# A graph layer on one core: the head's order on three engines, later node loads behind the edge list, paired stores, and GNN weights loaded in the adjacency

## The chip, the cores and the metric

The kernel runs on one core of one Trainium2 chip. The metric is device time in microseconds (us). The kernel before took 1140.14 us, the median of three runs (1139.82 to 1141.01). The engines are named as the profile names them: PE is TensorE (PEld its weight loads), DVE is VectorE, ACT is ScalarE, POOL is GpSimd, SP is SyncE, which here only issues transfers. ACTq and SPq are the transfer-issuing sides of ACT and SP.

## The reference, cut to what matters

One layer of a graph network for N = 3125 nodes of C = 256 numbers and E = 103,125 directed edges, sorted by destination. `xn` is the layer norm of `x`. The GNN part, the part that the change touches:

```
agg  = segment_sum(xn[src], dst, N)
h    = relu(agg @ W_rel + b_rel + xn @ W_root)
g    = h @ W_ih.T + b_ih + b_hh;  i, f, g, o = split(g, 4)
gnn  = (sigmoid(o) * tanh(sigmoid(i) * tanh(g))) @ W_fc + b_fc
x    = x + gnn + mix(xn)           # mix: per-head k'v attention, heads of 32
x    = x + ffn(layernorm(x))       # top 2 of 8 experts, 256 -> 1024 -> 256
```

## The kernel before, in words

Nodes lie in 25 tiles of P = 126 rows, five tiles to a batch (five batches, b = 0 to 4) and four to a root group (seven groups, r = 0 to 6, the last of one tile). The program has four stages: the head, the adjacency, the GNN, and the experts.

**The head** does two things at once.

*The edge list.* `dst` and `src` lie on the chip as 128 x 808 integers (`raw`). `find()` (L237) casts them on ACT (L248), transposes them on PE (L254), copies them out on ACT (L258, L261) and stores them to DRAM as `ends_dram` with two transfers issued by ACT (L263, 768 KB; L265, 42 KB). Meanwhile DVE counts for each of 525 groups of six destinations how many first entries of `firsts` lie below its limit (L275, five passes), which gives `at_i`. POOL gathers five blocks `near` with it (L283), DVE refines the position to `begin_i` (L289, L292), POOL gathers five blocks `both` of 256 edges per group (L297), DVE turns them into a key and a source row (L307 to L316), and checks the order of the list (L321, L322, L324). PE sums the check (L326), transposes the keys (L336), ACT writes `rowT` (L338) and DVE `keyT` (L340).

*The nodes.* `norm(b)` (L345) takes the moments of five tiles on DVE (L194, L195), a square root on ACT (L197, `rs`), a reciprocal and five scalings on DVE (L198, L349), and stores `xn_dram`. `rounded(b)` (L354) makes `hi`, the rounded copy, on ACT (L356); DVE makes `lo`, the rest (L436). `root(t0)` (L358) transposes four tiles on PE (L366, 8 transposes), copies them to `xt` on ACT (L368, two copies), multiplies by W_root on PE (L373: 8 matmuls of 504 columns, which the trace shows as 16), evacuates each of four results on ACT with the bias (L376, `hr`), and stores `xT_dram` (504 KB) and `root_dram` (four stores of 252 KB).

**The adjacency.** `build()` (L379) makes 18 columns of a 126 x 25 x 252 block A of the adjacency matrix: two comparisons on DVE (L384, `hr` and `hk`), six small matmuls on PE (L390), a cast on ACT (L392). A chunk needs 14 such banks. The comparisons have two buffers, so DVE is at most two banks ahead of PE. The first block, A0, is built in the head; PE begins chunk 0 of the aggregation (L631) when all 14 banks of A0 are there, and during chunk c builds the block for c + 1. There are 13 chunks. `fetch`, `means` and so on (L509 to L563) put the mix part between the banks.

**What sets the order.** Each engine runs its instructions in the order in which the compiled program has them. That order is chosen by the scheduler of the Tile framework, from the order in the source and from `tc.issue_after(ins)`, which puts what is written inside it behind `ins`. Every transfer issued by SP or ACT signals its end on one of eight semaphores, taken in turn by both queues together; before a transfer is issued, its queue waits until the transfer that had this semaphore before, the eighth before it in that turn, has landed. In the kernel before, the second list store (L265) has the semaphore of the first node batch, `xn` b = 0. Behind it on ACT stand the table load and the `rs` of that batch.

SP's order in the head before: `raw` (two loads), `xn` b = 0, `wroot`, `firsts`, `brel`, `xn` b = 1 to 4, `behind`, then twelve small loads (`wcol` to `of`), then the stores of the head with the loads of the GNN weights (L445 `wrel`, L450 `wih`, L452 `wfc`, 4 MB in all) among the last of them.

Of the kernel before, what the change touches and what calls it, by code (L numbers as in the profile page):

```python
# [9 lines left out]
F32 = mybir.dt.float32  # L10
# [3 lines left out]
AF = mybir.ActivationFunctionType  # L14
OP = mybir.AluOpType
# [3 lines left out]
C = 256  # L19
P = 126  # L20
# [43 lines left out]
def gps_layer(  # L64
# [35 lines left out]
    xT_dram = dram.tile([128, KC, NP], F32, name="xT_dram")  # L100
    root_dram = dram.tile([128, KH, NP], F32, name="root_dram")
# [13 lines left out]
    def load_nodes(to, t0, t1):  # L115

        if t1 == T:
            nc.vector.memset(to[:, T - 1 - t0, :], 0.0)
            nc.sync.dma_start(to[:LAST, T - 1 - t0, :], x[(T - 1) * P:N, :])
            t1 = T - 1  # L120
        if t1 > t0:
            nc.sync.dma_start(to[:, :t1 - t0, :], tiles_of(x, t0, t1))
# [32 lines left out]

    nc.sync.dma_start(raw[:, 0, :], dst)
    nc.sync.dma_start(raw[:, 1, :], src)
    for b in range(T // TB):
        load_nodes(xn[:, b * TB:(b + 1) * TB, :], b * TB, (b + 1) * TB)
        if b == 0:  # L160
            nc.sync.dma_start(wroot, W_root.rearrange("(k p) m -> p k m", p=128))
            nc.sync.dma_start(firsts, dst[0:1, :].to_broadcast([GP, NCP]))
            brel = columns_of(b_rel, KH, "brel")

    nc.sync.dma_start(behind[:112, :], dst[1:113, :])
    nc.sync.dma_start(behind[111:127, :], dst[112:, :])
    nc.sync.dma_start(behind[127:, :NCP - 1], dst[0:1, 1:])
# [48 lines left out]

    wcol = gw.tile([128, 2, KC], F32, name="wcol")
    for i, ap in enumerate((kln_w, kln_b)):
        nc.sync.dma_start(wcol[:, i, :], ap.rearrange("(k p) -> p k", p=128))
    wrow = gw.tile([128, 2, KC, 128], F32, name="wrow")  # L220
    for i, ap in enumerate((vln_w, vln_b)):
        nc.sync.dma_start(wrow[:, i].rearrange("p k c -> p (k c)"), rows_of(ap, C, 128))
    bfc = gw.tile([P, 1, C], F32, name="bfc")
    nc.sync.dma_start(bfc[:, 0, :], rows_of(b_fc, C, P))
    bg = columns_of(b_ih, 4 * KH, "bg").rearrange("p (g k) -> p g k", g=4)
    bg2 = columns_of(b_hh, 4 * KH, "bg2").rearrange("p (g k) -> p g k", g=4)
    wr = gw.tile([128, KC, NE], F32, name="wr")
    nc.sync.dma_start(wr, Wr.rearrange("(k p) e -> p k e", p=128))
    brb = gw.tile([P, 1, NE], F32, name="brb")
    nc.sync.dma_start(brb[:, 0, :], rows_of(br, NE, P))  # L230
    small = gw.tile([128, KS, NE], F32, name="small")
    ofs = [columns_of(ap, NE * k, f"of{k}{i}")
           for i, (ap, k) in enumerate(((ln_g, KC), (ln_b, KC), (b1, KF)))]

    total_i = const.tile([128, 1], I32, name="total_i")

    def find():  # L237
# [8 lines left out]
        for i in range(2):  # L246
            ends = sp.tile([128, NCP], F32, name="ends", tag="ends", bufs=2)
            nc.scalar.copy(ends, raw[:, i, :])  # L248
            for r in range(0, nr, 4):
                pt = ps_tr()  # L250
                m = min(4, nr - r)
                for j in range(m):
                    w = min(128, NCP - 128 * (r + j))
                    nc.tensor.transpose(pt[:w, 128 * j:128 * j + 128],  # L254
                                        ends[:, 128 * (r + j):128 * (r + j) + w], ident)
                whole_ = m if NCP >= 128 * (r + m) else m - 1
                if whole_:
                    nc.scalar.copy(rows[:, r:r + whole_, :, i],  # L258
                                   pt[:, :whole_ * 128].rearrange("p (r e) -> p r e", e=128))
                if whole_ < m:  # L260
                    nc.scalar.copy(rows[:left, r + whole_, :, i],  # L261
                                   pt[:left, whole_ * 128:m * 128])
# [10 lines left out]
        scr = sp.tile([GP, NCP], F32, name="scr", tag="ends", bufs=2)  # L273
# [18 lines left out]
        nc.vector.scalar_tensor_tensor(begin_i, at, 128.0, below, op0=OP.mult, op1=OP.add)  # L292
# [27 lines left out]
        order = sp.tile([128, NCP], F32, name="order", tag="ends", bufs=2)  # L320
# [3 lines left out]
        nc.vector.tensor_reduce(wrong[:, 1:2], full, AX.X, OP.add)  # L324
# [7 lines left out]
        for q in range(GQ):  # L332
            pt = ps_tr()
            for o, of in enumerate((g_src, key)):
                for h in range(GH):
# [4 lines left out]
            nc.vector.tensor_scalar(keyT[:, q * GP:(q + 1) * GP, :],  # L340
                                    pt[:, GH * GP:2 * GH * GP].rearrange("p (h g) -> p g h", h=GH),
                                    off, None, op0=OP.add)
# [15 lines left out]
    def root(t0):  # L358
# [10 lines left out]
        nc.sync.dma_start(xT_dram[:, :, t0 * P:t0 * P + n], xt[:, :, :n])  # L369
        for m in range(KH):  # L370
            pm = ps_mm()
            for k in range(KC):
                nc.tensor.matmul(pm[:, :n], wroot[:, k, 128 * m:128 * m + 128], xt[:, k, :n],  # L373
                                 start=(k == 0), stop=(k == KC - 1))
            hr = np_.tile([128, TQ * P], F32, name="hr", bufs=6)
            nc.scalar.activation(hr[:, :n], pm[:, :n], AF.Identity, bias=brel[:, m:m + 1])  # L376
            nc.sync.dma_start(root_dram[:, m, t0 * P:t0 * P + n], hr[:, :n])
# [25 lines left out]

    pins = []
    steps = find()
    next(steps)
    with tc.issue_after(pins.pop().ins):
        normed = norm(0)
    with tc.issue_after(normed.ins):
        next(steps)  # L410
    root(0)
    rounded(0)
    with tc.issue_after(pins.pop().ins):
        norm(1)
    next(steps)
    nc.vector.tensor_copy(two[:, 0], two_f[:, :, None].to_broadcast([128, DT, GH]))
    root(TQ)
    rounded(1)
    norm(2)
    root(2 * TQ)  # L420
    rounded(2)
    for _ in steps:
        pass
    norm(3)
    rounded(3)
    norm(4)
    rounded(4)
# [3 lines left out]
    root(3 * TQ)  # L431
    for _ in range(2):
        next(parts)
    for b in range(T // TB):
        u = slice(b * TB, b * TB + TB)
        nc.vector.tensor_tensor(lo[:, u, :], xn[:, u, :], hi[:, u, :], OP.subtract)  # L436
    for t0 in range(4 * TQ, T, TQ):
        root(t0)
        for _ in range(5):
            next(parts, None)  # L440
    nodes.close()
# [3 lines left out]
    nc.sync.dma_start(wrel, W_rel.rearrange("(k p) m -> p k m", p=128))  # L445
    wih = gl.tile([128, KH, 3, DH], F32, name="wih")

    wv = W_ihT.rearrange("(k p) m -> p k m", p=128)
    for i, gate in enumerate((0, 2, 3)):
        nc.sync.dma_start(wih[:, :, i, :], wv[:, :, gate * DH:(gate + 1) * DH])  # L450
    wfc = gl.tile([128, KH, C], F32, name="wfc")
    nc.sync.dma_start(wfc, W_fc.rearrange("(k p) m -> p k m", p=128))  # L452

# [6 lines left out]
    nc.sync.dma_start(wr_dram, wrT)  # L460

# [127 lines left out]
    def inputs(t0):  # L589
# [3 lines left out]
        nc.sync.dma_start(xT[:, :, :n], xT_dram[:, :, t0 * P:t0 * P + n])  # L593
        root = inp.tile([128, KH, TQ * P], F32, name="root", bufs=1)
        nc.sync.dma_start(root[:, :, :n], root_dram[:, :, t0 * P:t0 * P + n])
# [13 lines left out]
    with tc.tile_pool(name="odd", bufs=1) as op_:  # L609
        As = [A0, op_.tile([P, T, AC], F32R, name="A1")]  # L610
        for c, (d0, d1) in enumerate(chunks):
# [26 lines left out]
            for k in range(KC):  # L638
                nc.scalar.copy(aggT[:, k, d0:d1], pg[k][:, :n])  # L639
            if c == 2 * nb_ + 1:  # L640
# [542 lines left out]
```

## Time and profile before

| stretch of the profiled execution, us from the span's start | PE busy | DVE busy | ACT busy |
|---|---|---|---|
| 0 to 17.17, up to the first root matmul | 5.50 of 17.17 | 7.14 | 8.68 |
| 17.17 to 50.30, up to the check of the list (L326) | 27.63 of 33.13 | 25.82 | 12.91 |
| 50.30 to 59.04, up to the end of the last keyT | 5.11 of 8.74 | 8.38 | 3.60 |
| 59.04 to 97.03, up to the first matmul of chunk 0 | 35.06 of 37.99 | 19.46 | 21.17 |
| 97.03 to 116.00, chunk 0 | 18.38 of 18.97 | 16.73 | 7.58 |
| 116.00 to 324.80, chunks 1 to 10 | 198.20 of 208.80 | 169.08 | 128.13 |
| 324.80 to 740.00, the last chunks, the GNN, the routing | 387.67 of 415.20 | 229.38 | 142.45 |
| 740.00 to 1141.50, the experts | 379.43 of 401.50 | 78.54 | 102.72 |

The profiled execution took 1143.33 us, of which 1141.5 are the span from the first to the last instruction. A busy time is the sum over an engine's instructions in that stretch. A line of the profile names the source line (L373), the engine, the operation, what it writes and reads, and in brackets how long the engine had been idle before it and what released it. PEclk is the share of the full TensorE clock that was granted.

### The profile page before, as it was taken

How to read it: one execution, taken by the hardware profiler on the slowest of the kernel's cores; microseconds unless marked ns; L12 is line 12 of the kernel's file. 1: busy time of each engine (PE TensorE's matmuls, PEld its weight loads, DVE VectorE, ACT ScalarE, POOL GpSimd, SP SyncE). 2: the span in 40 equal slices, each digit the busy share in tenths (PEclk: the TensorE clock that was granted, in tenths of full speed). 3: DMA queues.
4: the chain of work that ended last, by engine and by line, in shares of the span. 5: the costliest groups of instructions: out<-in, count | busy, mean ns of one | idle time of the engine just before them, and what ended most of it. 6: DMA issues, size and time to landing. Idle time of an engine off the chain costs nothing. (4 is left out here: it accounts for less than half of the span.)

```text
span 1141.5 us, 15590 instructions
## 1 busy us (share of the span) xinstructions
PE 1057.0 (93%) x5613; PEld 808.4 (71%) x5613; DVE 554.5 (49%) x1772; ACT 427.2 (37%) x936; POOL 171.0 (15%) x157
## 2 busy tenths in 40 slices
PE   5799999999999999999999998199999998999995
PEld 2358988998996454545454548188888887888884
DVE  5857788778761184848383836501122221222111
ACT  3454755755732233333333336032222222223221
POOL 2220000000001002020202021212221221221222
PEclk9899999999999999999999999599999998999998
DMA  7893965963007421312121111247677776667771
GB/s 227 299 295 119 253 169 136 250 173 94 1 1 249 168 91 38 91 38 91 38 91 37 36 37 34 65 111 219 193 194 190 226 194 200 179 182 216 196 219 37
DMA packets 121101, 162.10 MB, mean 142 GB/s; under 512 B 9650, under 2 KB 109016, under 8 KB 120822
## 3 DMA queue, kind: packets, MB, share of 16 engines
q1 hardware_dynamic: 108300, 144.53, 41.3%
q0 software_dynamic: 11872, 15.60, 7.0%
q8 instruction: 50, 0.82, 0.3%
q10 hardware_dynamic: 840, 0.83, 0.2%
q14 instruction: 39, 0.32, 0.1%
HBM read 101.89 MB, written 62.23 MB: 144 GB/s over the span
## 5 line engine op out<-in xcount | busy, mean ns | idle before, releaser
L748 PE MATMUL ps_mm<-hT,wih 128*128 128x504 f32 (+1 forms) x672 | 257.8, 543 | 1.6 <-ACT act L750 1.6
L748 PEld LDWEIGHTS ps_mm<-hT,wih 128*128 128x128 f32 x672 | 120.5, 190 | 133.9 <-issue 127.5
L1054 PE MATMUL ps_mm<-xe,w 128*128 128x256 f32 (+1 forms) x896 | 191.2, 372 | 2.7 <-DVE xe L1048 2.7
L1067 PE MATMUL ps_o<-w,hf 128*128 128x256 f32 x832 | 184.2, 379 | 0.0
L1054 PEld LDWEIGHTS ps_mm<-xe,w 128*128 128x128 f32 x896 | 163.1, 194 | 26.7 <-DVE xe L1048 5.8
L631 PE MATMUL ps_o<-A,hi 126*128 126x252 f32 (+1 forms) x650 | 174.9, 303 | 0.8 <-ACT A L392 0.6
L1067 PEld LDWEIGHTS ps_o<-w,hf 128*128 128x128 f32 x832 | 158.0, 190 | 21.1
L631 PE MATMUL ps_o<-A,lo 126*128 126x252 f32 (+1 forms) x650 | 159.8, 279 | 0.0
L1056 ACT ACTIVATE hf<-ps_mm,sm 128x256 f32<-128x256 f32 (+1 forms) x160 | 71.5, 452 | 200.7 <-PE ps_mm L1054 199.0
L392 ACT CAST A<-ps_mm 126x450 fp32r<-126x450 f32 x175 | 93.6, 538 | 99.3 <-PE ps_mm L390 97.7
L631 PEld LDWEIGHTS ps_o<-A,hi 126*128 126x128 f32 x650 | 123.7, 190 | 3.0 <-ACT aggT L639 1.9
L384 DVE TENSOR_TENSOR hr<-two,rowT 128x756 bf16<-128x756 bf16 x175 | 95.7, 547 | 62.1 <-PE ps_mm L390 61.5
L631 PEld LDWEIGHTS ps_o<-A,lo 126*128 126x128 f32 x650 | 124.1, 191 | 0.0
L980 POOL DMA_INDIRECT acc_dram<-y,xs x48 | 74.2, 1546 | 298.6 <-DVE scr L1063 131.8
L390 PE MATMUL ps_mm<-hk,hr 128*126 128x150 bf16 x1050 | 102.3, 233 | 12.6 <-DVE hk L384 12.4
L384 DVE TENSOR_TENSOR hk<-two,keyT 128x900 bf16<-128x900 bf16 x175 | 108.5, 620 | 0.0
L390 PEld LDWEIGHTS <-hr 128*126 128x126 bf16 x1050 | 91.5, 138 | 18.6 <-DVE hk L384 16.4
L1070 DVE TENSOR_TENSOR y<-ps_o,b2s 128x256 f32<-128x256 f32 x52 | 22.0, 424 | 160.1 <-PE ps_o L1067 160.1
L750 ACT ACTIVATE act<-ps_mm,bg 128x504 f32<-128x504 f32 (+1 forms) x84 | 52.5, 633 | 107.4 <-PE ps_mm L748 104.6
L796 DVE SCALAR_TENSOR_TENSOR scr<-xl,wrows 126x256 f32<-126x256 f32 x160 | 75.7, 473 | 3.3
L873 POOL DMA_INDIRECT xs_dram<-rows,at_i x50 | 52.6, 1051 | 128.5 <-DVE at_i L870 111.4
L1056 ACT ACTIVATE hf<-ps_mm,small 128x256 f32<-128x256 f32 x64 | 29.9, 473 | 76.3 <-PE ps_mm L1054 75.9
(258 smaller groups left out, 931.1 us busy)
## 6 DMA issues: line engine op xcount, KB each, us to landing
w<-in_W_dram SPq DMA_DIRECT2D x56, 1024.0 KB
xs_dram<-blank SPq DMA_DIRECT2D x3, 7022.5 KB
xs_dram<-blank SPq DMA_DIRECT2D x1, 6757.5 KB
xs<-xs_dram SPq DMA_DIRECT2D x24, 265.0 KB
root_dram<-hr SPq DMA_DIRECT2D x24, 252.0 KB
root<-root_dram SPq DMA_DIRECT2D x6, 1008.0 KB
b2s<-in_b_dram SPq DMA_DIRECT2D x28, 128.0 KB
xn_dram<-xn SPq DMA_DIRECT2D x5, 630.0 KB
```

Source lines behind the costliest of these rows:

```text
L384: row = nc.vector.tensor_tensor(to[:, :m], two[:, :, :w, :].to_broadcast([128, m, w, GH]), of[:, g:g + m, None, :].to_broadcast([128, m, w ...
L390: mm = nc.tensor.matmul(pa[:P, i * DT:(i + 1) * DT], hr[:, i, :, h], hk[:, i, :, h], start=(h == 0), stop=(h == GH - 1))
L392: copy = nc.scalar.copy(A[:, :, c0:c0 + m * D], pa[:P, :m * DT].rearrange("p (d t) -> p t d", t=T))
L631: last = nc.tensor.matmul(pg[k][:, :n], of[:, t, 128 * k:128 * k + 128], A[:, t, :n], start=(t == 0 and of is hi), stop=(t == T - 1 and of ...
L748: mm = nc.tensor.matmul(pm[:, :n], wih[:, k, i, 128 * m:128 * m + 128], hT[:, k, :n], start=(k == 0), stop=(k == KH - 1))
L750: nc.scalar.activation(act[:, i, :n], pm[:, :n], AF.Tanh if gate == 2 else AF.Sigmoid, bias=bg[:, gate, m:m + 1])
L796: nc.vector.scalar_tensor_tensor(scr, xl[:, i, :], 1.0, wrows[:, e, :], op0=OP.mult, op1=OP.mult, accum_out=lg[:, i, e:e + 1])
L873: put = nc.gpsimd.indirect_dma_start(out=xs_dram[:, :], out_offset=bass.IndirectOffsetOnAxis(ap=at_i[:w, i:i + 1], axis=0), in_=rows[:w, i ...
L980: nc.gpsimd.indirect_dma_start(out=acc_dram[:, :], out_offset=bass.IndirectOffsetOnAxis(ap=of[:, h, C + NE:].bitcast(I32), axis=0), in_=y, ...
L1054: nc.tensor.matmul(pm, w1[:, k, 128 * m:128 * m + 128], xe[:, k, :], start=(k == 0), stop=(k == KC - 1))
L1056: nc.scalar.activation(hf[:, m, :], pm, AF.Gelu, bias=b1s[:, m:m + 1])
L1067: mm = nc.tensor.matmul(po, hf[:, m, 128 * h:128 * h + 128], w2[:, m, :], start=(m == 0), stop=(m == KF - 1))
```

## The change

The edits, as they stand in the source and in the compiled program:

- **Loads.** `firsts` goes ahead of `raw`. Batches 0 and 1 of the nodes are loaded at once. Batch 2 waits for the landing of the second list store, and batches 3 and 4, `behind` and `wr` are put after it. The other eleven small loads move in the source to the end of the head; in the compiled program SP issues them directly behind batch 1, and ahead of batch 2. In the turn of the eight semaphores the second list store (now L246) comes after `wcol` of `kln_b`, the second of the small loads.
- **Order.** The counts for `at_i` come ahead of `norm(0)` on DVE. Three buffers instead of two serve the tag `ends`. `norm` and `rounded` are put behind chosen instructions. PE runs root groups 0 to 3 and the first half of group 4 before the check of the list (L309) and the key transposes (L319), the other half of 4 between these, and groups 5 and 6 between the first banks. On ACT the order is: list store, table load, `rs` 0, `hi` 0, `xt` 0, `rs` 1, four `hr`, `rs` 2, `xt` of group 1, four `hr`, `hi` 1, `rs` 3, `xt` of group 2, four `hr`, `hi` 2, `xt` of group 3, four `hr`, `hi` 3, `xt` of group 4, and so on. On DVE, `begin_i` is followed by `norm(2)`, `norm(3)`, the keys, the moments of batch 4, `keyT`, two banks, `lo` of four batches, three banks, the last `lo`, and nine banks.
- **Stores.** `xT_dram` and `root_dram` get a layout by root group, and two results of a group are stored by one transfer (504 KB, runs of 4032 bytes instead of 2016). The loads of them in the GNN follow the layout.
- **GNN weights.** `wrel`, `wih` and `wfc` are loaded after chunk 1 of the aggregation instead of in the head.

```diff
@@ loads
+    nc.sync.dma_start(firsts, dst[0:1, :].to_broadcast([GP, NCP]))
     nc.sync.dma_start(raw[:, 0, :], dst)
     nc.sync.dma_start(raw[:, 1, :], src)
-    for b in range(T // TB):
-        load_nodes(xn[:, b * TB:(b + 1) * TB, :], b * TB, (b + 1) * TB)
-        if b == 0:
-            nc.sync.dma_start(wroot, W_root.rearrange("(k p) m -> p k m", p=128))
-            nc.sync.dma_start(firsts, dst[0:1, :].to_broadcast([GP, NCP]))
-            brel = columns_of(b_rel, KH, "brel")
-    nc.sync.dma_start(behind[:112, :], dst[1:113, :])
...
+    load_batch(0)
+    nc.sync.dma_start(wroot, W_root.rearrange("(k p) m -> p k m", p=128))
+    brel = columns_of(b_rel, KH, "brel")
+    load_batch(1)
@@ find()
-            ends = sp.tile([128, NCP], F32, name="ends", tag="ends", bufs=2)
+            ends = sp.tile([128, NCP], F32, name="ends", tag="ends", bufs=3)
@@ root()
+            if m % 2 == 0:
+                hr = np_.tile([128, 2, TQ * P], F32, name="hr", bufs=3)
+            evac = nc.scalar.activation(hr[:, m % 2, :n], pm[:, :n], AF.Identity,
+                                        bias=brel[:, m:m + 1])
+            evacs.append(evac)
+            if m % 2:
+                store = nc.sync.dma_start(root_dram[:, t0 // TQ, m - 1:m + 1, :n], hr[:, :, :n])
+            if between and m == KH // 2 - 1:
+                with tc.issue_after(mm.ins):
+                    between()
@@ the head
+    later = load_batch(2)
+    tc.add_manual_dep(later.ins, listed.ins.name, ... reason="the list first")
+    with tc.issue_after(later.ins):
+        for b in range(3, T // TB):
+            load_batch(b)
+        nc.sync.dma_start(behind[:112, :], dst[1:113, :])
...
+    next(steps)
+    last = then(pins.pop(), norm, 0)
     root(0)
     rounded(0)
+    last = then(last, norm, 1)
+    then(last, next, steps)
+    last = behind_((pins.pop(), evacs[-1]), norm, 2)
+    root(TQ)
+    then(evacs[-1], rounded, 1)
+    last = behind_((last, evacs[-1]), norm, 3)
+    root(2 * TQ)
+    then(evacs[-1], rounded, 2)
+    root(3 * TQ)
+    then(evacs[-1], rounded, 3)
+    then(last, next, steps)
+    listed = pins.pop()
+    root(4 * TQ, lambda: next(steps, None))
+    behind_((listed, evacs[-3]), norm, 4)
+    then(evacs[-1], rounded, 4)
+    found.close()
+    parts = builds(A0, 0)
+    for t0, n, m in ((5 * TQ, 3, 4), (6 * TQ, 0, NB)):
+        root(t0, lambda: [next(parts) for _ in range(n)])
+        for _ in range(m):
+            next(parts, None)
     with tc.issue_after(pins.pop().ins):
+        for b in range(T // TB):
+            u = slice(b * TB, b * TB + TB)
+            nc.vector.tensor_tensor(lo[:, u, :], xn[:, u, :], hi[:, u, :], OP.subtract)
@@ the adjacency, end of a chunk
+            if c == 1:
+                wv = W_ihT.rearrange("(k p) m -> p k m", p=128)
+                loads = [nc.sync.dma_start(wrel, W_rel.rearrange("(k p) m -> p k m", p=128)),
...
+                for load in loads:
+                    tc.add_manual_dep(load.ins, last.ins.name, ... reason="later")
```

## The prediction

> **What bounds the kernel now.** I read the table of stretches first: from chunk 0 on, nothing that the change touches has PE idle, and the chain of waits behind PE in the head (0 to 97.03 us) holds all that can move. Then PE in order of time:
>
> ```profile
> 5.17 3.55 PE L254 MATMUL ps_tr<-ident,ends 128*128 128x128 f32 x14 [5.17 <-ACT ends L248]
> 14.16 2.02 PE L366 MATMUL ps_tr<-ident,xn 126*128 126x126 f32 x8 [5.44 <-DVE xn L349]
> 17.17 8.58 PE L373 MATMUL ps_mm<-xt,wroot 128*128 128x504 f32 x16 [0.99 <-ACT xt L368]
> 28.41 1.47 PE L366 MATMUL ps_tr<-ident,xn 126*128 126x126 f32 x7 [2.55 <-DVE xn L349]
> 32.09 9.64 PE L373 MATMUL ps_mm<-xt,wroot 128*128 128x504 f32 x16 [2.22 <-ACT xt L368]
> 43.02 7.03 PE L373 MATMUL ps_mm<-xt,wroot 128*128 128x504 f32 x16 [0.43 <-ACT xt L368]
> 50.30 0.36 PE L326 MATMUL ps_tr<-wrong,ones 128*128 128x2 f32 x2 [0.26 <-DVE wrong L324]
> 59.99 7.58 PE L373 MATMUL ps_mm<-xt,wroot 128*128 128x504 f32 x16
> 80.89 6.96 PE L373 MATMUL ps_mm<-xt,wroot 128*128 128x504 f32 x16
> 97.03 0.39 PE L631 MATMUL ps_o<-A,hi 126*128 126x252 f32 x1 [0.65 <-ACT A L392]
> ```
>
> The reader sees seven root groups (16 passes each, 0.42 us apart at full clock, so 6.8 us) around the list check at 50.30. After the last key (59.04) PE is busy 35.06 of 37.99 us while DVE needs only 19.46: the second half is bound by PE, the first by what PE waits for. Next, ACT around the list store, and SP's loads:
>
> ```profile
> 9.17 0.39 ACTq L263 DMA_DIRECT2D ends_dram<-rows  x1
> 10.81 0.57 ACTq L265 DMA_DIRECT2D ends_dram<-rows  x1
> 11.41 1.28 ACT L197 ACT_TABLE_LOAD   x1 [2.13 <-DMA xn<-in_x_dram]
> ...
> SPq L122 <- DMA firsts<-in_dst_dram: 1.2, 1, 1.2
> SPq L219 <- DMA xn<-in_x_dram: 0.9, 1, 0.9
> ```
>
> The second list store is held until `xn` of batch 0 has landed (10.8), because the two share a semaphore; the table load and the first `rs` (13.09) are held with it. SP's waits date two landings: it issues the next load at 15.03, after waiting for `firsts`, and at 20.93, after waiting for `xn` of batch 2. Last, the clock beside PE's busy time:
>
> ```profile
> 27.40:30.80 3.40, 1.41 (x7) 0.80 (x7) 3.35 (x17) 1.07 (x1) 1.24 (x2) 0.97 0.55 137
> 30.80:34.20 3.40, 2.11 (x3) 1.10 (x4) 2.60 (x13) 2.02 (x5) 0.84 (x3) 0.50 0.57 119
> 88.80:92.30 3.50, 2.12 (x20) 1.80 (x21) 3.50 (x8) 1.93 (x5) 0.00 (x0) 0.96 0.65 237
> 92.30:95.70 3.40, 3.40 (x21) 3.40 (x20) 1.10 (x3) 1.53 (x5) 0.00 (x0) 0.54 0.15 44
> ```
>
> The first number after the comma is PE's busy time, the last but two the granted clock: after a stretch that is 41% or 61% busy, the next one has half the clock.
>
> **The change part by part.** I go along the path that sets the first matmul of chunk 0.
>
> *1. The list store's wait.* It now shares its semaphore with the second small load (`wcol`), which stands on SP's queue behind `xn` of batch 1. Ahead of batch 1 stand the same loads as before, only in another order, so it follows the 15.03 of `firsts`; two batches later is 20.93, which puts batch 1 at 18.0, and the two small loads of 256 pieces add some 0.3: 18.3, with 15.0 and 20.9 as ends. Before it was 10.81. The store takes 0.57 and the table load 1.28, so the first `rs` comes at 18.3 + 1.9 = 20.2 instead of 13.09, 7.1 later, and with it scalings, `hi`, `xt` and root group 0: 17.17 + 7.1 = 24.3. `firsts` ahead of `raw` costs the list itself about 1.3 (331 KB beside the 404 KB that take from 0.75 to 4.16), hidden in this wait. The early counts (5 x 1.13 us on DVE) also end, at 10.3, inside it. Batches 2 to 4 are held too: SP waits for the list's landing (about 21), so batch 2 lands near 25, before DVE wants it at 31.
>
> *2. The position.* `near` can go when the list has landed, about 20.5 (before 22.73, behind the counts); five gathers of 1.27 and 3.5 us to landing give 30.3, `begin_i` 30.8 (before 33.85). ACT now has `rs` of batch 2 ahead of group 1's `xt`; its moments (5 x 0.48) follow `begin_i`, so 33.7. What is queued behind it: the `xt` for which PE waits.
>
> *3. Root groups 0 to 4a.* Group 0 with a cold clock as before, 8.6: 32.9. Group 1: transposes 1.0, `xt` 0.6, 34.5; 6.8 gives 41.3. From here ACT has `hi` (1.26) between the last evacuation and the next `xt`: release 0.25 + 0.6 + 1.26 + 0.55 + 0.25 = 2.9 us from PE's last root pass to its next, of which transposes fill 1.0. Before, between groups 1 and 2 it was 43.02 - 41.7 = 1.3. So groups 2 and 3 end at 51.0 and 60.7, the first half of 4 (2.9 + 3.4) at 67.0. There stands the list check, 16.7 later than 50.30, with 1.5 more groups done. The keys are ready long before: DVE has norms 2 and 3 (4.8 each), then keys (11.2), from 31 to 52.
>
> *4. Keys.* Before 8.74 to the last `keyT`, with 2.5 of it spent by `total_f` behind moments on DVE. Now about 6.9, and the rest of group 4 runs in the gaps: 73.9.
>
> *5. Building A0.* What remains for PE, groups 5 and 6 and 14 banks, is 17 us; DVE is now the bound: a scaling 0.35, 14 banks at 1.01 (starts 90.32 and 91.32 of two `hr`) and five `lo` at 1.43, less the first `hr`: 21.2. It stops 2.5 where PE has root work ahead of banks (3.4 of group 5, 1.8 or more of group 6, two banks of lead), and the last bank takes 1.3 on PE and ACT: 25.0, so chunk 0 begins at 98.9, 1.9 later than 97.03.
>
> *6. The clock.* Groups 0's 1.7 is counted on both sides, and 97.03 contains what was lost at 30.8, 54.7 and 92.3. The new gaps are not: 2.9 us with 1.0 of transposes leaves a 3.4 us stretch 45 to 70% busy. Here the Trainium skill speaks (TensorE: Matmul & The Clock Gate, "Why this matters for your kernels"): only gaps of more than about 3 us between bursts cost the clock. By the rule none of these counts and the sum stays at +1.9. The row 88.80:92.30 says otherwise: no gap in it is over 0.8 us, it is 61% busy, and the next stretch has half the clock. I follow the row. Each such stretch costs 1.7 of root work; there are four such gaps (before groups 2, 3, 4 and 5) and the start of chunk 0 after banks at half load. I take two and a half of the five: +4.1. Bounds 0 and 8.5.
>
> *7. At nothing.* Paired stores: before, evacuations waited only 1.06 and 2.11 us for a store, both between 39 and 50 with the queues at 360 GB/s; three pairs hold what six singles held, and a root group now takes 9.7 us for 2.2 MB of stores, about 6 at that rate. Without that cover an evacuation would wait for up to one pair, 1.4. GNN weights: 4 MB leave a head in which no wait after 59 is for a store. In the adjacency they follow the first 7 MB fill (116 to 145 at 254 GB/s) for 16 us, to about 162; on SP's queue behind them stands the third `fetch`, issued at 151.17, whose mean is taken at 193. Cover 31 us; without it the bank behind that mean is late by what is missing. Wider reads in the GNN: PE is at 100% there. Small loads: `bg` reaches POOL's addition, which now stands ahead of `near`, at about 20.3; the list lands at 20.5.
>
> Sum: +1.9 + 4.1 = +6.0 on the profiled span, 1141.5 to 1147.5 (1149.3 with the 1.8 around it). The median of the runs is 3.2 under that execution's 1143.33; the same shift gives 1140.14 + 6.0 = 1146.1.
>
> **The rivals.** A difference under 0.2% (2.3 us) is what a measurement of this kernel can't tell from none.
>
> *Faster: the store's wait ends early.* One mechanism: the small load lands with batch 0 (about 12.3) instead of behind batch 1. Then `rs` comes at 14.5, group 0 at 18.7, and steps 2 to 5 move by as much until DVE's list work binds: chunk 0 at 92.7, and with one half-clock stretch 94.4, which is 1137.5. [...] Against it: [...] SP's waits show landings in order of issue. It decides from below 12.7 with 1.7 of clock, below 14 with none.
>
> *No change.* The wait ends at 16 or 17 and the clock holds, as the skill's rule has it: 98.9 - 1.9 = 97.0, 1140. For it: gaps of 1.3 to 2.3 us at 41.7 and 67.4 cost no clock. Against it: those had banks or transposes in them for most of their length.
>
> *Slower still.* The later loads become the bound: batch 2 waits for the list and meets stores; if its moments come 5 us after 31, `rs` 2 holds group 1's `xt` by that, and all five gaps cost clock: +6 + 5 + 3 = 1154. Against it: SP has the queue to itself at 21.
>
> **How the numbers follow.** Main case (1142.5 to 1152) 0.56, faster 0.22, no change 0.12, slower still 0.10. Faster 0.22, same 0.12, slower 0.66. The likeliest time is 1146.1. Of the wait's ends, 15.0 takes 3.3 off and 20.9 adds 2.6; of the clock's, -4.1 and +4.4. The range is 1137 to 1153, leaving out part of the faster and of the slowest case; the main case alone has 1142.5 to 1152.
>
> **What would show it.** Right: the second list store at 17 to 20, the table load behind it; group 0 at 23 to 26; 2.5 to 3.5 us between groups with `hi` before `xt`; the list check at 65 to 73; DVE busy from the last `keyT` to chunk 0; half clock in several head stretches; chunk 0 at 99 to 107, and no change in the length of later chunks. Wrong: a list store before 14; or a first `xt` of group 2 right after the last evacuation; or a time gained in the adjacency or GNN, where I expect none.

## The result

The changed kernel takes 1144.77 us, the median of 20 runs (1141.29 to 1151.75), beside 1140.69 us for the kernel before on the same chip (20 runs, 1136.15 to 1143.99). The ratio is 1.0036 with a 95% interval of 1.0024 to 1.0049: slower by 4.1 us. The profiled execution took 1145.05 us, with a span of 1143.2.

PE in order of time in the profile after, start and busy time first, the idle time before it and what ended it in brackets (the root passes and the marks of the head; the transposes between them are left out):

```profile
16.62 2.02 PE L353 MATMUL ps_tr<-ident,xn 126*128 126x126 f32 x8 [6.37 <-ACT rs L197]
19.63 10.10 PE L360 MATMUL ps_mm<-xt,wroot 128*128 128x504 f32 x16 [0.99 <-ACT xt L355]
32.72 8.68 PE L360 MATMUL ps_mm<-xt,wroot 128*128 128x504 f32 x16 [2.13 <-ACT xt L355]
43.98 7.03 PE L360 MATMUL ps_mm<-xt,wroot 128*128 128x504 f32 x16 [1.72 <-ACT xt L355]
53.41 7.03 PE L360 MATMUL ps_mm<-xt,wroot 128*128 128x504 f32 x16 [1.54 <-ACT xt L355]
62.84 3.65 PE L360 MATMUL ps_mm<-xt,wroot 128*128 128x504 f32 x8 [1.53 <-ACT xt L355]
66.32 0.28 PE L309 MATMUL ps_tr<-wrong,ones 128*128 128x2 f32 x2
...
93.17 0.64 PE L385 MATMUL ps_mm<-hk,hr 128*126 128x150 bf16 x6 [0.36 <-DVE hk L379]
...
96.80 0.58 PE L660 MATMUL ps_o<-A,hi 126*128 126x252 f32 x1
```

Group 0 comes 2.5 us later than before (17.17), the list check 16.0 later, and in the last stretch the banks wait for DVE (L385, "hk"), as predicted. Yet chunk 0 begins at 96.80, where it began at 97.03. Its first pass is booked with 0.58 us instead of 0.39: PE is at half clock. The first copy out of chunk 0 starts at 117.5 instead of 116.0.

The list store on ACT and on ACT's queue, in order of time:

```profile
10.70 0.40 ACTq L244 DMA_DIRECT2D ends_dram<-rows  x1
13.65 0.57 ACTq L246 DMA_DIRECT2D ends_dram<-rows  x1
14.25 1.28 ACT L197 ACT_TABLE_LOAD   x1 [3.43 <-DMA wcol<-in_kln_b_dram]
```

The wait is the one foretold: ACT stands still for 3.43 us until a 1 KB load on the other queue has landed. It is shorter: the store goes at 13.65, not at 18.3. DVE, in order of time, has two large holes that it did not have before. One, of 7.19 us up to 43.50, is a wait for ACT's `rs`; the larger is this:

```profile
66.64 0.16 DVE L311 TENSOR_REDUCE total_f<-ps_tr 128x1 f32<-128x2 f32 x1 [10.28 <-PE ps_tr L309]
```

For 10.28 us DVE waits for the list check on PE, which stands behind four and a half root groups; what it checks is ready on DVE at 54.3. Last, busy time and clock in stretches (PE, its weight loads, DVE, ACT, POOL; then the clock, the DMA share and GB/s), cut at the places where the clock changes in this execution:

```profile
29.26:32.67 3.41, 1.33 (x10) 0.82 (x8) 2.97 (x15) 1.45 (x4) 1.73 (x2) 1.00 0.98 377
32.67:36.08 3.41, 3.36 (x4) 1.51 (x5) 3.41 (x14) 0.48 (x1) 2.50 (x4) 0.50 0.94 295
...
59.98:63.39 3.41, 1.88 (x12) 1.13 (x11) 0.00 (x0) 2.79 (x4) 0.00 (x0) 1.00 0.37 151
63.39:66.80 3.41, 3.41 (x13) 1.78 (x12) 0.16 (x1) 0.96 (x2) 0.00 (x0) 1.00 0.37 154
...
90.70:94.11 3.41, 1.90 (x18) 1.43 (x18) 3.41 (x8) 1.64 (x4) 0.53 (x3) 1.00 0.27 58
94.11:97.53 3.42, 3.17 (x17) 2.59 (x18) 3.22 (x9) 1.35 (x3) 0.00 (x0) 0.50 0.90 309
97.53:100.94 3.41, 3.41 (x19) 3.41 (x18) 0.67 (x2) 0.54 (x1) 0.00 (x0) 0.50 0.28 87
```

The gap before root group 1 (first row) is followed by half clock, and that group takes 8.68 us where the next ones take 7.03. The gap before group 4 (third row) leaves the clock full, the DVE-bound banks (fifth row) halve it, although PE's busy time is the same. That half clock lasts into chunk 0 up to 100.9.

So the two profiles differ at the end of chunk 0 by 1.5 us. The rest of the adjacency takes 2.3 us longer (239.2 instead of 236.9), what follows it 2.2 less, and in the whole they differ by 1.7, while the medians differ by 4.1. One execution of each kernel doesn't settle where the time is lost. The experiments had to.

### The profile page after: what moved, and what is told of

Its sections match the earlier page's. It is cut to its first block, busy times and chain, and to the rows that moved or that the text cites. A ratio compares the mean times of both kernels' runs of the same rounds, so it can differ in the third digit from the quotient of the medians.

```text
span 1143.2 us, 15562 instructions
## 1 busy us (share of the span) xinstructions
PE 1056.9 (92%) x5613; PEld 809.4 (71%) x5613; DVE 555.9 (49%) x1772; ACT 427.8 (37%) x936; POOL 165.4 (14%) x157
## 5 line engine op out<-in xcount | busy, mean ns | idle before, releaser
L660 PE MATMUL ps_o<-A,hi 126*128 126x252 f32 (+1 forms) x650 | 179.0, 308 | 0.0
L660 PE MATMUL ps_o<-A,lo 126*128 126x252 f32 (+1 forms) x650 | 164.1, 284 | 0.0
L660 PEld LDWEIGHTS ps_o<-A,hi 126*128 126x128 f32 x650 | 127.0, 195 | 1.7 <-ACT aggT L668 1.5
L660 PEld LDWEIGHTS ps_o<-A,lo 126*128 126x128 f32 x650 | 127.5, 196 | 0.0
L385 PE MATMUL ps_mm<-hk,hr 128*126 128x150 bf16 x1050 | 103.9, 234 | 14.2 <-DVE hk L379 13.3
L385 PEld LDWEIGHTS <-hr 128*126 128x126 bf16 x1050 | 92.4, 139 | 20.2 <-DVE hk L379 18.8
```

Of the source, the lines that this page charges most:

```text
L385: mm = nc.tensor.matmul(pa[:P, i * DT:(i + 1) * DT], hr[:, i, :, h], hk[:, i, :, h], start=(h == 0), stop=(h == GH - 1))
L660: last = nc.tensor.matmul(pg[k][:, :n], of[:, t, 128 * k:128 * k + 128], A[:, t, :n], start=(t == 0 and of is hi), stop=(t == T - 1 and of ...
```

## The experiments

My theory was the prediction's: ACT's order (the list store's wait, `hi` ahead of `xt`) and the DVE-bound banks lengthen the head, and the clock at the start of chunk 0 adds to it. The rivals: these waits are absorbed by one another; the loss lies behind chunk 0 (GNN weights, the clock in the adjacency); it lies in the stores.

### The second list store early

```diff
-    wcol = gw.tile([128, 2, KC], F32, name="wcol")
-    ... the other small loads
+    with tc.issue_after(later.ins):
+        wcol = gw.tile([128, 2, KC], F32, name="wcol")
+        ... the other small loads
-    nc.gpsimd.tensor_tensor(bg, bg, bg2, OP.add)
+    with tc.issue_after(found_.ins):        # the last step of the list on DVE
+        nc.gpsimd.tensor_tensor(bg, bg, bg2, OP.add)
```

> The changed kernel with the eleven small loads put behind the later node batches, so that the second list store shares its semaphore with firsts, which lands early. If the list store's wait is still on the path to chunk 0 (3.4 us of ACT in the changed kernel), the store goes at about 11.1 instead of 13.65, the first rs at 13.2 instead of 15.55, root group 0 at 17.3 instead of 19.63, begin_i at about 27 instead of 29.7, the list check at 63 to 64 instead of 66.3, and chunk 0 begins at 93.5 to 94.5 instead of 96.8: about 1142. If the wait is absorbed behind it (slack in the list's own work, or the half clock of the first 26 us), group 0 comes earlier but chunk 0 stays within 1 us of 96.8, and the time stays at 1144 to 1145.

Measured: 1142.99 us beside 1140.17, ratio 1.0025 (1.0012 to 1.0037). ACT's queue and PE in order of time:

```profile
11.73 0.70 ACTq L246 DMA_DIRECT2D ends_dram<-rows  x1
...
17.84 8.67 PE L360 MATMUL ps_mm<-xt,wroot 128*128 128x504 f32 x16 [0.99 <-ACT xt L355]
31.71 8.56 PE L360 MATMUL ps_mm<-xt,wroot 128*128 128x504 f32 x16 [4.34 <-ACT xt L355]
...
95.68 0.58 PE L662 MATMUL ps_o<-A,hi 126*128 126x252 f32 x1
```

Without the wait the first `rs` comes at 13.76 instead of 15.55 and group 0 1.8 us earlier. Group 1 then idles 4.34 us instead of 2.13, because its `xt` stands behind the `rs` of batch 2, and that behind `begin_i`. 1.0 us is left at group 1 and 1.1 at chunk 0. In these two executions both theories are half right: something over half of what the wait costs at group 0 reaches chunk 0. But chunk 0's start differs by up to 3 us between executions of the changed kernel alone (the table under the cut kernels), so a difference of 1.1 between one execution of each is an indication only. The median is 1.1 parts in 1000 lower than that of the changed kernel, which the intervals don't separate.

### `hi` behind the next `xt`

```diff
-    def root(t0, between=None):
+    def root(t0, between=None, behind_xt=None):
...
-            nc.scalar.copy(xt[:, k, :n], pt[:, :n])
+            copied = nc.scalar.copy(xt[:, k, :n], pt[:, :n])
+        if behind_xt is not None:
+            then(copied, rounded, behind_xt)
...
-    then(evacs[-1], rounded, 1)
-    root(2 * TQ)
+    root(2 * TQ, None, 1)               # and so on for batches 2, 3 and 4
```

> The changed kernel with hi of batches 1 to 4 put behind the xt copies of the next root group on ACT, instead of ahead of them. If the four gaps of 2.6 us between root groups are on the path, they shrink to 1.3 to 1.5, the list check comes at 61 to 62.5 instead of 66.3, and chunk 0 at 91.5 to 93 instead of 96.8: about 1140.5. If the end of the head is set by DVE's banks whatever PE does before, or hi then delays the evacuations by as much, chunk 0 stays at 96 to 97 and the time at 1144 to 1145.

Measured: 1141.12 us, ratio 1.0001 (0.9986 to 1.0016). PE in order of time:

```profile
41.27 7.03 PE L362 MATMUL ps_mm<-xt,wroot 128*128 128x504 f32 x16 [0.56 <-ACT xt L355]
51.28 8.72 PE L362 MATMUL ps_mm<-xt,wroot 128*128 128x504 f32 x16 [2.12 <-ACT xt L355]
61.24 3.65 PE L362 MATMUL ps_mm<-xt,wroot 128*128 128x504 f32 x8 [0.38 <-ACT xt L355]
64.73 0.28 PE L309 MATMUL ps_tr<-wrong,ones 128*128 128x2 f32 x2
72.09 3.65 PE L362 MATMUL ps_mm<-xt,wroot 128*128 128x504 f32 x8 [0.38 <-ACT xt L355]
...
94.02 0.58 PE L658 MATMUL ps_o<-A,hi 126*128 126x252 f32 x1
```

Before groups 2, 4 and 5 the idle times of 1.72, 1.53 and 1.54 us become 0.56, 0.38 and 0.38; only that before group 3 grows, from 1.54 to 2.12. ACT in order of time shows why:

```profile
44.95 0.68 ACT L366 ACTIVATE hr<-ps_mm,brel 128x504 f32<-128x504 f32 x1 [1.01 <-PE ps_mm L362]
49.51 1.25 ACT L366 ACTIVATE hr<-ps_mm,brel 128x504 f32<-128x504 f32 x2 [3.87 <-DMA root_dram<-hr]
```

With the groups closer together the evacuations reach the three buffers of the paired stores too early, and one waits 3.87 us for a store. The gap of 2.12 us that this opens before group 3 is followed by half clock (0.50 from 52.61 to 56.02), and the group takes 8.72 us instead of 7.03. In the changed kernel's profile group 1 lost as much; here it takes 7.03, so the two cancel. Chunk 0 begins 2.8 us earlier, at 94.02, not at 91.5 to 93 as expected, and the median is where it was before the change: 0.0035 in the ratio, 4.0 us, hangs on the place of four casts on ACT, and the two intervals do not meet. The profiled execution is the longest of the fourteen, so it cannot show where all of the 4.0 us lies. Chunk 0 still begins at half clock.

### The list check in group 3

```diff
-    root(3 * TQ)
-    then(evacs[-1], rounded, 3)
     then(last, next, steps)
     listed = pins.pop()
-    root(4 * TQ, lambda: next(steps, None))
+    root(3 * TQ, lambda: next(steps, None))
     behind_((listed, evacs[-3]), norm, 4)
+    then(evacs[-1], rounded, 3)
+    root(4 * TQ)
     then(evacs[-1], rounded, 4)
```

> The changed kernel with the list check and the key transposes in the middle of root group 3 instead of group 4. DVE is idle from 56.4 to 66.6 in the changed kernel with the keys ready at 54.2; if that wait costs the end of the head, the check comes at 56.5 to 57.5, the last keyT at about 62, lo of four batches is done before group 5, DVE has 5 to 6 us less to do behind it, and chunk 0 begins at 91.5 to 93.5, with PE denser among the last banks: about 1140. If PE bounds the end, chunk 0 stays at 96 to 97: 1144 to 1145.

Measured: 1143.54 us, ratio 1.0022 (1.0010 to 1.0035). PE in order of time:

```profile
33.55 7.03 PE L360 MATMUL ps_mm<-xt,wroot 128*128 128x504 f32 x16 [2.98 <-ACT xt L355]
...
56.25 0.28 PE L309 MATMUL ps_tr<-wrong,ones 128*128 128x2 f32 x2
...
86.58 1.99 PE L360 MATMUL ps_mm<-xt,wroot 128*128 128x126 f32 x16
...
95.80 0.58 PE L660 MATMUL ps_o<-A,hi 126*128 126x252 f32 x1
```

The check comes 10 us earlier, chunk 0 only 1.0. The expectation of 91.5 to 93.5 failed. Even the 1.0 need not be the check's: group 1 happens to run at full clock here (first line; 8.68 us in the changed kernel's profile), and two executions with the check in its old place and full clock in group 1 began chunk 0 at 95.79 (the next experiment) and 96.00 (the changed kernel cut off behind the adjacency). From group 6 to chunk 0 it is 9.2 us, as in the changed kernel (87.59 to 96.80): the banks still stand in groups 5 and 6, the comparisons have two buffers, and so, as I read it, DVE can't begin the later banks sooner just because the keys are there sooner. The place of the banks on PE must move as well.

### Banks that keep PE busy

```diff
-        for i in range(m):
+        for i in (*range(again), *range(m)):     # again = 2 for the last seven banks of A0, else 0
             for h in range(GH):
                 mm = nc.tensor.matmul(pa[:P, i * DT:(i + 1) * DT], hr[:, i, :, h], hk[:, i, :, h],
```

> The changed kernel with four of the six matmuls of each of the last seven banks of A0 done twice, so that PE is about 85% busy there instead of half; the results are the same. If the half clock at the start of chunk 0 comes from PE's low load among the DVE-bound banks, the granted clock is full from about 91 on, chunk 0 begins at about the same 96.8, its first copy out comes at about 115.9 instead of 117.5, and the time is 1.3 to 1.7 less: about 1143.2. If that clock was chance, or the banks become slower by the extra work, nothing is gained: 1144.5 to 1146.

Measured: 1144.12 us, ratio 1.0035 (1.0023 to 1.0047). Stretches of the profile:

```profile
88.00:91.40 3.40, 2.83 (x37) 2.51 (x36) 2.50 (x5) 2.02 (x5) 0.53 (x3) 1.00 0.26 76
91.40:94.80 3.40, 2.93 (x36) 2.45 (x34) 3.38 (x8) 1.75 (x4) 0.00 (x0) 1.00 0.63 201
94.80:98.20 3.40, 3.32 (x32) 3.09 (x30) 2.60 (x7) 1.08 (x2) 0.00 (x0) 1.00 0.64 222
```

The clock is full throughout, and chunk 0 takes 18.5 us (95.79 to 114.3) instead of 20.7. In the seven other profiles with this order of the banks (the changed kernel three times, the first three experiments, and the longer gap below) chunk 0 begins at half clock. So PE's low load among the banks is the cause of the half clock at the start of chunk 0. The stretch from group 6 to chunk 0 is 0.4 longer, which leaves 1.8 to be had; the median shows none of it, and the intervals, some 2.8 us wide, neither prove nor exclude it.

### The kernel before again

> The kernel before, unchanged, profiled a second time. Its first profiled execution was 3.2 us over the median of its runs and had five half-clock stretches of 3.4 us between 30 and 96 us. If the changed kernel loses its time in the head, that first execution was a slow one for the head: here the first copy out of chunk 0 comes at 112.5 to 114.5 instead of 116.0, with two to four such stretches. If the loss lies behind chunk 0, it comes at 116 again, and what follows takes less than the 1025.5 us of the first execution. The ratio is 1.000 either way.

Measured: 1141.67 beside 1141.47, ratio 1.0002 (0.9987 to 1.0016). PE in order of time:

```profile
51.30 0.35 PE L326 MATMUL ps_tr<-wrong,ones 128*128 128x2 f32 x2 [3.14 <-DVE wrong L324]
...
97.82 0.39 PE L631 MATMUL ps_o<-A,hi 126*128 126x252 f32 x1 [0.65 <-ACT A L392]
```

Chunk 0's first copy comes at 116.8, not at 112.5 to 114.5: the first profile of before was no odd one in the head. There is half clock in six stretches of the head, and none in chunk 0.

### Stores and weights alone

The kernel before with the diff's parts for paired stores, the layout and the GNN weights, and nothing else.

> The kernel before with only two parts of the change: paired stores with the new layout, and the GNN weights loaded after chunk 1. If both are worth nothing, as the prediction has it, the ratio is 0.999 to 1.001 and no wait for a load shows in chunks 2 to 5. If the weights push the third fetch behind its cover of 31 us, or an evacuation waits for a pair of stores, 1 to 3 us are lost: 1.001 to 1.003.

Measured: 1143.43 beside 1141.47, ratio 1.0025 (1.0005 to 1.0045), from twelve runs between 1141.01 and 1152.46; the profiled execution was the fastest of them. ACT in order of time:

```profile
46.49 0.30 ACT L198 ACTIVATE rs<-mv,eps 126x5 f32<-126x5 f32 x1 [6.59 <-DVE mv L196]
46.69 1.23 ACT L378 ACTIVATE hr<-ps_mm,brel 128x504 f32<-128x504 f32 x2
48.22 0.68 ACT L378 ACTIVATE hr<-ps_mm,brel 128x504 f32<-128x504 f32 x1 [0.30 <-DMA root_dram<-hr]
```

The last line is what the stores were suspected of: an evacuation waits 0.30 us for a pair, where it waited 2.11 us for a single store at this place before. No other wait for a store came up. The 6.59 us in the first line are a wait for DVE, which itself waits 2.26 us for a block of gathered edges (0.71 at most before), and PE loses 2.60 us in group 2 by it; whether the paired stores slow that gather is not shown. The list check still comes at 50.68 (before 50.30), chunk 0 begins at 96.24 (before 96.41 to 97.82), and in the adjacency the stalls have their lengths of before (0.50, 0.17 and 1.74 us in each pair of chunks). Still the median is 2.0 us up, with an interval that only just excludes no change; two of the twelve runs, at 1149.99 and 1152.46, carry about half of the excess. The profile, of the fastest run, doesn't show where; whether these two parts cost something stays open.

### A longer gap

```diff
-        nc.scalar.copy(hi[:, s, :], xn[:, s, :])
+        for _ in range(2 if 0 < b < 4 else 1):
+            nc.scalar.copy(hi[:, s, :], xn[:, s, :])
```

> The changed kernel with hi of batches 1 to 3 made twice, so that PE's idle time before groups 2, 3 and 4 grows from 1.5 to 1.7 us to 2.7 to 2.9 us, behind 1.0 us of transposes. The four stalls of 1.74 us in the adjacency are followed by half clock where they fall whole into one 3.4 us stretch of the clock's grid, and not where the grid cuts them. If idle time above 1.7 us within such a stretch is what counts, two or three of the three gaps now cost the clock, each 1.7 us, and chunk 0 comes at 3.4 + 3.4 to 5.1 later than in the changed kernel: about 103 to 105. If only idle times of more than about 3 us count, there is no half clock after these gaps: about 100.

Measured: 1150.04 beside 1141.47, ratio 1.0069 (1.0040 to 1.0098), five runs between 1146.21 and 1153.93. Only the first gap grew. In the others the second cast fell between the two `xt` copies, and PE began as before. Stretches cut at this execution's clock grid:

```profile
40.73:44.14 3.41, 1.59 (x10) 0.93 (x8) 0.55 (x3) 2.65 (x4) 0.00 (x0) 1.00 1.01 401
44.14:47.55 3.41, 2.35 (x6) 1.19 (x7) 3.41 (x17) 1.84 (x4) 0.00 (x0) 1.00 0.74 273
```

PE idles 2.88 us before group 2, 1.82 of it in one stretch, and the clock stays full. Before group 1, which the edit doesn't touch, it idles 3.27 us, 2.26 of it in one stretch (30.47 to 33.88), and the clock halves: the group takes 8.72 us. Chunk 0 begins at 98.03. Both expectations for it were wrong (103 to 105, 100), the first because the clock didn't drop behind the gap that grew, both because one gap grew instead of three. The profile's head explains 1.2 us over the changed kernel; the median is higher by more, which I can't place.

### The repairs together

The edits of the first three experiments in one kernel, and the banks spread over three root groups:

```diff
-    for t0, n, m in ((5 * TQ, 3, 4), (6 * TQ, 0, NB)):
+    behind_((keyed, last), rest, 0, 1, 2)        # lo of batches 0 to 2 behind the keys
+    for t0, n, m, b in ((4 * TQ, 2, 3, 3), (5 * TQ, 3, 4, 4), (6 * TQ, 0, NB, None)):
```

> The changed kernel with the three repairs together: small loads behind the later batches, hi behind the next xt, the list check and keys in group 3; further lo of three batches ahead of the banks, and the banks spread over groups 4, 5 and 6. If PE's work bounds the head then, the check comes at about 53, group 4 at 60 to 61, and chunk 0 at 88 to 90: 1134 to 1136. If DVE's banks or ACT's order of evacuations bound it, chunk 0 comes at 92 to 94, and the time is 1138 to 1140.

Measured: 1134.6 us beside 1141.47, ratio 0.9935 (0.9909 to 0.9960): faster than both kernels. PE in order of time:

```profile
53.20 0.28 PE L309 MATMUL ps_tr<-wrong,ones 128*128 128x2 f32 x2
...
60.56 3.65 PE L362 MATMUL ps_mm<-xt,wroot 128*128 128x504 f32 x8 [0.38 <-ACT xt L355]
65.57 3.58 PE L362 MATMUL ps_mm<-xt,wroot 128*128 128x504 f32 x8
71.28 3.58 PE L362 MATMUL ps_mm<-xt,wroot 128*128 128x504 f32 x8
76.94 3.58 PE L362 MATMUL ps_mm<-xt,wroot 128*128 128x504 f32 x8
83.59 1.99 PE L362 MATMUL ps_mm<-xt,wroot 128*128 128x126 f32 x16
...
87.06 0.38 PE L665 MATMUL ps_o<-A,hi 126*128 126x252 f32 x1 [0.65 <-ACT A L389]
```

From 53.20 to chunk 0 PE is busy 30.76 of 33.86 us. Chunk 0 begins 9.7 us earlier than in the changed kernel, at full clock, and its first copy comes at 106.1 instead of 117.5. That is 11.4 us; the ratios differ by 0.0101, 11.5 us. The rest of the adjacency is no shorter (239.4 us). The parts alone, one execution each, moved chunk 0 by 1.1, 2.8 and 1.0 us; the other 4.8 I put down to the spread banks with the earlier `lo`, which were not tried alone.

### Both kernels cut off

Each kernel ended behind chunk 0, and each ended behind the adjacency:

```diff
             for k in range(KC):
                 nc.scalar.copy(aggT[:, k, d0:d1], pg[k][:, :n])
+            break                                # the first cut; the second has it behind the loop
```

> The kernel before, ended after chunk 0: everything behind the first two copies out of chunk 0 is left out, also the 7 MB fill, and the output is filled with chunk 0's result. Read together with the same cut of the changed kernel. In the profiles chunk 0's first copy came at 116.0 and 116.8 (before, two executions) and at 117.5 (changed). If the 4 us are lost by then, the medians of the cut kernels differ by 3.5 to 4.5 us; if half of them are lost behind chunk 0, by 0.7 to 2.

> The changed kernel with the same cut. Against the cut kernel before: 3.5 to 4.5 us more if all is lost in the head and chunk 0, 0.7 to 2 us more if part of it is lost in the adjacency.

> The kernel before, ended after the last chunk of the adjacency: the GNN, the routing and the experts are left out, and the output is filled with the aggregated columns. In the profiles the adjacency ended at 352.9 and 353.7 (before) and 356.7 (changed), with one half-clock stretch behind chunk 0 before and three after the change. If the loss is complete here, the medians of the two cut kernels differ by 3.3 to 4.5 us; if the GNN or the experts hold a part of it, by 2 or less.

> The changed kernel with the same cut behind the adjacency. Against the cut kernel before: 3.3 to 4.5 us more if all is lost by here, and 2 us or less more if the GNN or the experts hold a part of it. If it is more than at the cut behind chunk 0 by 1.5 to 2.5 us, the adjacency's extra half-clock stretches are no accident of one execution.

| ended behind | before, us | changed, us | difference of the medians |
|---|---|---|---|
| chunk 0 | 151.66 (151.13 to 153.87, 6 runs) | 155.19 (151.17 to 156.15, 6 runs) | +3.5 |
| the adjacency | 381.05 (379.45 to 382.68, 5 runs) | 385.03 (384.21 to 385.27, 5 runs) | +4.0 |
| the whole | 1140.69 (20 runs) | 1144.77 (20 runs) | +4.1 |

By the end of the adjacency all is lost: there the runs of the two kernels do not overlap, and the GNN and the experts add nothing. Behind chunk 0 the medians say that nearly all is lost by then, and that the adjacency adds 0.5, but this is less sure. Five of the changed kernel's six runs lie at 154.45 to 156.15; the sixth, at 151.17, is as short as the kernel before. The profiled execution (155.62 us) is one of the five. It shows ACT waiting longer than in the first profile. ACT and PE in order of time:

```profile
16.62 0.61 ACTq L246 DMA_DIRECT2D ends_dram<-rows  x1
17.27 1.28 ACT L197 ACT_TABLE_LOAD   x1 [5.41 <-DMA wcol<-in_kln_b_dram]
...
98.97 0.58 PE L660 MATMUL ps_o<-A,hi 126*128 126x252 f32 x1
```

Here the store goes 3.0 us later than in the first profile, group 0 starts at 22.68, and chunk 0 at 98.97. The cut kernel before was profiled at 151.23 us with chunk 0 at 96.41: 2.6 of the 4.4 us between these two executions lie before chunk 0, and 1.5 in it. There is no profile of the short run, so it is not shown that the store's wait is what sets the five apart.

| profiled execution | list store | chunk 0 begins | its first copy out | length |
|---|---|---|---|---|
| before, four executions | 9.6 to 10.8 | 97.03, 97.82, 96.41, 97.41 | 116.0, 116.8, 115.4, 116.4 | 19.0 each |
| changed, three executions | 13.65, 16.62, 14.04 | 96.80, 98.97, 96.00 | 117.5, 119.5, 116.4 | 20.7, 20.5, 20.4 |

## Why the prediction was right, and where it was not

Direction and size came out (1146.1 predicted, 1144.8 measured), but the size owes something to luck, because its terms did not. The sum was +6.0, +1.9 for chunk 0's start and +4.1 for the clock. Measured, the start moves by between -1.8 and +2.6 us, over the pairs of executions in the table, the clock costs 1.4 to 1.7 in chunk 0, and the profiles show 0.9 to 2.6 in the rest of the adjacency, for which the prediction had no change. Of its own signs of being right, the gaps, the list check and DVE busy before chunk 0 appeared. The list store (17 to 20), group 0 (23 to 26) and chunk 0 (99 to 107) came earlier than said in all three profiles of the changed kernel, and the store at 13.65 in the first of them is one of its signs of being wrong.

- *Step 1, the list store.* The mechanism was right: the wait for `wcol`, behind batch 1. Its size was not: 18.3 was predicted with 15.0 as the lower end, 13.65 measured, and 13.6 to 16.6 over all executions with this order. The term that failed is batch 1's landing at 18.0. In the profile after, SP issues a load at 13.18 that waited for this batch. I had dated it by landings of a queue in which three batches were issued together; in the new order only small loads stand behind batch 1. That this is why it lands early is not shown.
- *Step 2* gave `begin_i` at 30.8 (measured 29.65) and `rs` of batch 2 at 33.7 (31.90). The position is what group 1 waits for, and that is why step 1's error of 4.7 us is 1.8 at group 1 (34.5 predicted, 32.72).
- *Step 3.* The gaps of 2.9 us were 2.7 and 2.6, with `hi` ahead of `xt`. Group 0 took 10.10 us instead of 8.6, which the wait for the position took up; group 1 took 8.68 instead of 6.8, which cancels what step 2 had gained. So the check's 66.32 (67.0) is in part luck. The second experiment shows what `hi`'s place costs: as much as the change lost.
- *Step 4.* The last `keyT` ended at 71.75 and group 4 at 72.5 (73.9).
- *Step 5.* DVE bounds the banks, as said, and chunk 0's start of 98.9 is the latest of those measured (96.00, 96.80, 98.97).
- *Step 6* failed. Of five stretches at risk I counted two and a half at 1.7 us each (which is 4.25, not 4.1). In the first profile one of the five cost the clock, the start of chunk 0, and that by the load of the banks, as the fourth experiment shows. A gap that I had not put at risk, before group 1, cost it too. For the four gaps that I counted the rule of the Trainium skill that I set aside (TensorE: Matmul & The Clock Gate, "Why this matters for your kernels"), which warns of idle gaps over about 3 us, was the better guide: with 1.5 to 2.0 us idle they cost nothing in any of the three profiles. It does not carry further. Idle times of 2.13 us (group 1) and 2.12 us (group 3, second experiment) were followed by half clock, and 3.06 and 3.11 us (group 1, the cuts of the changed kernel) by full clock; among the banks no idle time in 90.70 to 94.11 exceeds 0.8 us, and the clock halved. The last section shows what went with it instead.
- *Step 7.* The weights delay nothing in the adjacency's profile: they are issued from 136.06 to 148.3, the third fetch at 152.37 (before 151.17), its mean is taken at 195.5, and the stall next to it has its 1.74 us as before. The stores wait for nothing in the changed kernel because its gaps cover them. With the gaps closed, in the second experiment, an evacuation waits 3.87 us; I had put 1.4 on that. Stores and weights alone, costed at nothing, measured +2.0 us; that is not explained. Nor is the longer adjacency: its stalls have their old lengths, but more of them are followed by half clock (last section).

Of the rivals, the faster one asked for a store before 14 with no clock lost. The store came at 13.65, clock was lost, and the kernel was slower: that rival passed each microsecond of the wait on to chunk 0 (and 0.6 more: its shift of 5.6 us gives 93.3, not 92.7), and the first experiment shows that the list's position takes up some of it. The rival of no change named 97.0 for chunk 0's start, and 96.80 came in the first profile, but not because the clock held: it was lost at group 1 and among the banks. The slower one, later loads as the bound, doesn't show: batch 2 is issued at 17.23 and its moments follow `begin_i` without a wait.

What stays open: the three profiles of the changed kernel account on average for 0.1 us at chunk 0's start and 1.5 in chunk 0, the cut kernels for 3.5. At the last copy out of the adjacency the profiles differ on average by 2.5 us (three of before, two of the changed kernel), the cut kernels by 4.0. How the loss divides between the head, chunk 0 and the adjacency is therefore not settled. One profile gives one execution, and the store's wait alone differs by 3 us between them.

## What to carry to other kernels

A cast that is needed late must not stand between the last evacuation of one group and the first copy of the next on the in-order engine that feeds PE; moving four such casts gained what the whole change had lost. When work is to fill another engine's gaps, look at the buffers between them: keys that were ready 10 us earlier moved chunk 0 by 1 us at most, and together with the banks spread over the root groups and two small repairs by 10. Where one execution's profile shows less than the medians do, cut both kernels at the same place and time the pieces.

## What the runs showed of the hardware that I had not expected

**The clock changes on a grid.** In each execution all its changes fall on multiples of 3.41 us from one offset, and the offset differs between executions of one kernel (0.4, 1.4, 3.1 and 3.3 us in the four profiles of before). So a stall can cost the clock in one execution and not in the next. The adjacency of both kernels has four stalls of this kind:

```profile
154.97 0.63 PE L385 MATMUL ps_mm<-hk,hr 128*126 128x150 bf16 x6 [1.74 <-DVE hk L379]
```

From chunk 0's first copy to the last one the adjacency takes 236.9 us where one of the four is followed by half clock (before, twice), 237.9 to 238.3 with two, and 239.2 to 239.5 with three (changed, twice): about 1.2 us each. The count hardly is chance alone: of the eight profiles with the new order that reach so far, experiments included, seven have three and one has two (the fourth experiment), while the kernel before has one, one and two. Why, these runs don't show.

**For the gaps between root groups, where the grid cuts one counts more than its length.** Take the stretches of the grid, from 25 us on, that hold a gap before a root group in the changed kernel and the experiments on it. With 0 to 1.33 us of busy time left in the stretch, half clock followed, five times: 1.33 before group 1 in the first profile, 1.33 before group 3 in the second experiment, 1.15 before group 1 with the longer gap, and nothing at all before group 1 with the list store early and with the repairs together. With 1.48 us or more the clock stayed full. The longest gap that cost nothing, 3.11 us before group 1 in the first cut, left 1.67 us in its stretch.

**Busy time alone does not foretell it.** In the second profile of the kernel before, a stretch with 1.69 us (24.30 to 27.72, the end of a root group and three transposes) was followed by half clock, so the bound above holds only for the executions that it was read from. Stretches of the grid with 1.88 us (59.98 to 63.39) and, with the longer gap, 1.59 us of PE's busy time were followed by full clock. One with 1.90 (90.70 to 94.11), and in the profile after one with 1.67 (152.13 to 155.54), by half clock. The two at full clock hold root passes and transposes, the last two banks, and banks and aggregation passes. In chunk 0 six matmuls of a bank, booked with 0.58 us, delay the next pass by only 0.38 (98.54 to 98.92 before), so the busy time overstates the banks; the 1.67 us of the last stretch this doesn't explain. What the clock counts, these runs don't settle.
